# The aggregates' part of a candidate gate as seven block products, with new planner durations and a scrap tile that goes

## Chip, cores and metric

One core of one Trainium2 chip runs the whole program. The metric is the time of one execution on the device, in microseconds (us); the kernel before takes 2567.4 us, the median of three runs (2566.71 to 2567.45). All data are 32-bit floats, the adjacency matrices integers.

## The reference

128 graphs of 128 nodes with 256 features pass three graph attention layers, each added to its input, and a gated graph network of three steps. Cut to what matters here:

```python
# three attention layers (W, a of their own)
h = jnp.maximum(_layernorm(x, axis=-1), 0.0)
Wh = jnp.einsum('bnf,fo->bno', h, W)
e = (Wh @ a1)[:, :, None] + (Wh @ a2)[:, None, :]
e = jnp.where(e > 0, e, ALPHA * e)
attention = softmax(jnp.where(adj > 0, e, NEG_BIG), axis=-1)
x = x + elu(jnp.einsum('bij,bjo->bio', attention, Wh))     # layer 2 also times the node mask

# the gated network
h = jnp.maximum(_layernorm(x, axis=-1), 0.0)
for i in range(3):
    m = jnp.einsum('bnd,de->bne', h, weight[i])
    aggr = jnp.einsum('bst,bsd->btd', A, m)                 # A = (adj != 0)
    i_r, i_z, i_n = split(aggr @ w_ih.T + b_ih)
    h_r, h_z, h_n = split(h @ w_hh.T + b_hh)
    r, z = sigmoid(i_r + h_r), sigmoid(i_z + h_z)
    n = tanh(i_n + r * h_n)
    h = (1.0 - z) * n + z * h
return x + h
```

## The kernel before

**Tiling.** The graphs are cut into 33 groups: two graphs in the first and the last, four in the others. A group of four has 4 x 128 = 512 columns. In the gated network the state lies with features on the 128 partitions, as two blocks of 128 features (`k`), and the nodes of the group along the columns; `H` is half of the columns, `D` = 256. Groups 2 to 30 turn tiles by a DVE transpose and a trip through DRAM (`exchanged`, `turned_state`), the first two and the last two by products with an identity on TensorE. Each group runs three attention layers (`attention`), then three steps of the gated network (`step`), then its output.

**A step.** `aggregate` sums the neighbours' states (`agp`), and ACT copies the sum into `ag`. The matrices `weight[i]` and `w_ih` are multiplied in the set-up, so that the gates use `WC[i]` on `ag` and `WHH` on the state `h`. A product of a 256 x 256 matrix with a 256 x 512 tile, which as plain blocks is eight products of 128 x 128 with 256 columns, is done with seven: the tile is cut into blocks, `sums` (DVE) makes four differences of them (`t13`, `t24`), the set-up's `combinations` (POOL) made the matching sums of the matrix blocks, and ACT and DVE add up the partial results between the products, inside PSUM banks. `gates` does so for r and z (banks `a`, `e`, `b`), for the state's part and the aggregates' part alike, both into the same banks. `hidden_n` does it for the state's part of the candidate (banks `nn`, `nnb`) and leaves it in `wn`. The aggregates' part of the candidate goes another way: `candidate(c)` has DVE write (r + 1) x `wn` into a bank `ni`, lets TensorE add two plain 512-wide products onto it, and takes the Tanh from there. `kept_share` and `mixed` (in the last step `last_mixed`) make the new state. The r gate is used as tanh of half its argument, hence the factors of 0.5 and 0.25.

**Banks and buffers.** PSUM has eight banks, dealt out in rings: "gat" 2 (attention), "gru" 3 (`a`, `e`, `nn`), "seed" 2 (`b`, `nnb`, `ni`), "tr" 1. A tile of a ring is taken in turn; who wants a tile waits until all users of the tile that had it before are done. `wn` has four buffers (two taken by each step, with the first product of `hidden_n`), the input and residual tile `x` six, `em` (the attention matrix) two; the products of the scores with the vectors `VA` need an output that nobody reads, `scr`, with two buffers of its own.

**The order.** Nothing is left to a scheduler of the compiler: the class `Plan` collects all operations with an engine, a cost in us, a rank (a due time) and what they read and write, then `issue` plays them through as if they ran and so sets the order of every engine's instructions and of SP's DMAs. On each engine it takes, of the operations that can start first (within `WINDOW`), the one of lowest rank; operations whose rank is more than `AHEAD` (`EARLY` while the lowest rank is below `UNTIL`) above the lowest one left are held back. `LAG` is the time from an operation's end on one engine to its user on another. `pe`, `dve`, `act` and `pool` give costs by column count. Ranks come from the tables `ATT` (a group's three layers and the entry into the gated network), `STARTS` (its three steps), beyond the tables from a period of 3.0 ranks a group, and `SETUPS` for the set-up. The instructions then run on the chip when their data are there, in that order on each engine. DMAs all go through SP's queue.

## Time and profile before

The profiled execution took 2566.74 us; its span, from the first to the last instruction, is 2565.0 us.

| view | what | value |
|---|---|---|
| runs | median of three | 2567.4 us |
| profiled execution | time / span | 2566.74 / 2565.0 us |
| granted clock of TensorE | mean over the span | 0.993 |
| busiest group of PE | `hp`, attention's second product | 356.2 us |
| next | `ni`, the aggregates' part of the candidate (L1047) | 352.9 us, 792 instructions |
| DVE | score products L610 | 270.3 us |
| ACT | Tanh of the candidate L1052, 512 wide | 127.7 us, 687 ns each |
| POOL | power for the norms L528, 4 wide | 137.9 us, 1112 ns each |
| chain that ended last | share of PE | 95% |
| DMA | mean rate over the span | 96 GB/s |

PE is TensorE, PEld its weight loads, DVE the vector engine, ACT the scalar engine, POOL GpSimd, SP the engine that issues the DMAs. A 32-bit product appears as two instructions in the trace. A row of a group reads: line, engine, operation, output <- inputs, shapes, count, then busy time and mean ns of one, then the engine's rest just before such an instruction and what ended it. A line of waits reads: who <- what ended the wait, us in all, how many times, the longest. The mean of one instruction is its own length; since instructions overlap in an engine's pipe, a queue of them is spaced more closely than that.

### The profile page before, as it was taken

What the parts mean: (1) busy time and instruction counts of PE and PEld (TensorE: products, weight loads), DVE (VectorE), ACT (ScalarE), POOL (GpSimd) and SP (SyncE); (2) the same over time, 40 slices, a digit from 0 to 9 for tenths busy, and PEclk for the clock granted to TensorE, in tenths of its full rate; (3) what the DMA queues carried; (4) which work ended last, traced back from release to release, by engine and by line L of the source; (5) the groups of instructions that cost most, each with busy time, mean ns of one, the idle gap of its engine ahead of it and who ended that gap; (6) DMA issues with size and microseconds to landing.
All of it is one profiled execution on the core that took longest, in us unless ns stands there. A gap on an engine that the chain in (4) does not pass through costs nothing.

```text
span 2565.0 us, 39018 instructions
## 1 busy us (share of the span) xinstructions
PE 2527.7 (99%) x12549; PEld 2098.6 (82%) x12549; DVE 2105.9 (82%) x4955; ACT 1768.5 (69%) x4411; POOL 225.1 (9%) x328
## 2 busy tenths in 40 slices
PE   8799999999999999999999999999999999999998
PEld 5688888888888888888888888888888888888887
DVE  6778888888888888888888888888888888888765
ACT  6777676776766776766776666776666777666554
POOL 2210000000000000000000000000000000000000
PEclk8899999999999999999999999999999999999999
DMA  3113343343343333343334333333334443333320
GB/s 106 46 57 97 87 111 108 95 108 95 106 109 99 107 104 95 108 107 103 105 102 96 109 104 106 104 100 100 107 103 104 107 99 101 101 89 97 75 62 13
DMA packets 503123, 245.75 MB, mean 96 GB/s; under 512 B 280579, under 2 KB 472067, under 8 KB 502918
## 3 DMA queue, kind: packets, MB, share of 16 engines
q1 hardware_dynamic: 502918, 243.25, 35.3%
q8 instruction: 100, 1.64, 0.3%
q14 instruction: 105, 0.86, 0.1%
HBM read 139.28 MB, written 103.87 MB: 95 GB/s over the span
## 4 chain that ended last, share of the span: by engine, by line
PE 95%; DVE 2%; ACT 2%; DMA 1%; issue 0%; SPq 0%; POOL 0%; ACTq 0%; DVEq 0%
PE b L965 19%; PE hp L742 13%; PE e L965 13%; PE ni L1047 13%; PE a L965 13%; PE ahp L723 7%; PE agp L991 6%; PE nn L952 6%; PE nnb L952 5%; ACT em L666 0%; DVE scr L610 0%; ACT em L679 0%; PE hnp L852 0%; DMA at<-d_at 0%; ACT hn L791 0%
## 5 line engine op out<-in xcount | busy, mean ns | idle before, releaser
L742 PE MATMUL hp<-w,ah 128*128 128x256 f32 x1536 | 356.2, 384 | 0.5 <-ACT ah L730 0.5
L1047 PE MATMUL ni<-ag,wc_n 128*128 128x512 f32 (+1 forms) x792 | 352.9, 580 | 0.9 <-DVE ni L1041 0.9
L742 PEld LDWEIGHTS hp<-w,ah 128*128 128x128 f32 x1536 | 286.7, 191 | 61.9 <-ACT ah L730 13.1
L610 DVE SCALAR_TENSOR_TENSOR scr<-xn,va 128x256 f32<-128x256 f32 x732 | 270.3, 418 | 36.1 <-ACT xn L602 35.8
L1047 PEld LDWEIGHTS ni<-ag,wc_n 128*128 128x128 f32 x792 | 147.1, 190 | 125.2 <-issue 104.0
L756 ACT ACTIVATE t<-hp 128x512 f32<-128x512 f32 x192 | 104.6, 595 | 201.3 <-PE hp L742 201.2
L1052 ACT ACTIVATE wn<-ni,bi 128x512 f32<-128x512 f32 (+1 forms) x198 | 133.4, 674 | 157.5 <-PE ni L1047 114.5
L991 PEld LDWEIGHTS agp<-am,hn 128*128 128x128 f32 x1536 | 204.7, 191 | 42.7 <-issue 30.8
L991 PE MATMUL agp<-am,hn 128*128 128x128 f32 x1536 | 208.9, 275 | 3.6 <-ACT ag L999 3.0
L525 POOL TENSOR_SCALAR ve<-st 128x4 f32<-128x4 f32 (+1 forms) x132 | 28.4, 215 | 2087.8 <-DVE st L519 1735.5
L965 PE MATMUL a<-h,whh_rz 128*128 128x256 f32 (+1 forms) x792 | 208.8, 373 | 0.8 <-ACT z L1035 0.5
L723 PEld LDWEIGHTS ahp<-at,xn 128*128 128x128 f32 x1536 | 190.6, 196 | 23.0 <-issue 14.4
L602 ACT ACTIVATE xn<-x,nm,rs 128x256 f32<-128x256 f32 x366 | 201.1, 594 | 3.8 <-DVE nm L531 3.8
L965 PE MATMUL a<-ag,wc_rz 128*128 128x256 f32 (+1 forms) x792 | 199.1, 373 | 0.0
L723 PE MATMUL ahp<-at,xn 128*128 128x128 f32 x1536 | 192.5, 279 | 4.6 <-DMA at<-d_at 2.8
L758 DVE SCALAR_TENSOR_TENSOR x<-hp,x 128x512 f32<-128x512 f32 x192 | 124.0, 685 | 71.0 <-ACT t L756 70.9
L519 DVE BATCH_NORM_STATS2 st<-x 128x6 f32<-128x512 f32 x256 | 170.3, 690 | 2.6 <-DMA x<-in_x_dram 2.5
L649 ACT ACTIVATE em<-er,e 128x128 f32<-128x128 f32 x366 | 164.3, 523 | 2.4 <-DMA er<-de 2.3
L666 ACT ACTIVATE em<-em,nmx 128x128 f32<-128x128 f32 x384 | 149.4, 392 | 11.6 <-DVE nmx L662 11.4
L965 PEld LDWEIGHTS a<-h,whh_rz 128*128 128x128 f32 x792 | 140.9, 191 | 16.9 <-issue 0.7
L965 PEld LDWEIGHTS a<-ag,wc_rz 128*128 128x128 f32 x792 | 141.1, 191 | 15.2 <-issue 0.5
L528 POOL TENSOR_TENSOR rs<-ve,mhalf 128x4 f32<-128x4 f32 (+1 forms) x132 | 144.0, 1091 | 11.0
(158 smaller groups left out, 5541.3 us busy)
## 6 DMA issues: line engine op xcount, KB each, us to landing
d_hn<-tr_hn SPq DMA_DIRECT2D x116, 256.0 KB, 2.4
hn<-d_hn SPq DMA_DIRECT2D x464, 64.0 KB, 2.3
er<-de SPq DMA_DIRECT2D x90, 256.0 KB, 3.9
d_at<-tr_at SPq DMA_DIRECT2D x90, 256.0 KB, 2.2
at<-d_at SPq DMA_DIRECT2D x360, 64.0 KB, 2.0
x<-in_x_dram SPq DMA_DIRECT2D x31, 512.0 KB, 5.0
d_h<-tr_h SPq DMA_DIRECT2D x31, 512.0 KB, 2.7
h<-d_h SPq DMA_DIRECT2D x124, 128.0 KB, 2.7
```

Source lines behind the costliest of these rows:

```text
L519: add("DVE", dve(T), rank, lambda: nc.vector.bn_stats(st.t[:, b, :].rearrange("p b s -> p (b s)"), xt.t[:, b, :].rearrange("p b d -> p d b ...
L528: add("POOL", 1.04, rank, lambda: nc.gpsimd.tensor_tensor(rs.t, ve.t, mhalf[:, :n], op=OP.pow), reads=[ve], writes=[rs])
L602: add("ACT", 0.45, rank, lambda: nc.scalar.activation(xn.t[:, b, :], xt.t[:, b, :], AF.Relu, bias=nm.t[:, b : b + 1], scale=rs.t[:, b : b ...
L610: add("DVE", dve(D), rank, lambda: nc.vector.scalar_tensor_tensor(scr.t, xn.t[:, b, :], 1.0 if far else rs.t[:, b : b + 1], VA[l].t[:, s, ...
L649: add("ACT", 0.55 if far else 0.42, rank, lambda: nc.scalar.activation(em.t[:, b, :], e2_row(b), AF.Prelu, bias=e.t[:, 0, b : b + 1], alph ...
L666: add("ACT", 0.42, rank, lambda: nc.scalar.activation(em.t[:, b, :], em.t[:, b, :], AF.Exp, bias=nmx.t[:, b : b + 1], accum_out=sm.t[:, b ...
L723: add("PE", pe(P), rank, lambda: nc.tensor.matmul(summed(ps, b), xn.t[:, b, k * P : (k + 1) * P], turned_weights(b), start=True, stop=True ...
L742: add("PE", pe(D), rank, lambda: nc.tensor.matmul(hp.t[:, b * D : (b + 1) * D], ah.t[:, k, c * P : (c + 1) * P], W[l].t[:, k, :], start=(k ...
L952: op = add("PE", pe(H), at, lambda: nc.tensor.matmul(ps.t[:, o : o + H], WHH[1].t[:, blk, :], rhs(), start=starts, stop=True, skip_group_c ...
L965: nc.tensor.matmul(ps.t[:, gate * D : gate * D + H], w[0].t[:, blk, gate * P : (gate + 1) * P], rhs(), start=go, stop=w is not WHH, skip_g ...
L991: nc.tensor.matmul(ps.t[:, b * P : (b + 1) * P], s, am.t[:, b, :], start=True, stop=True)
L1047: add("PE", pe(TG), rank + 0.45 + 0.05 * c, lambda k=k: nc.tensor.matmul(ni[c].t[:, :TG], WC[i][1].t[:, k, c * P : (c + 1) * P], ag.t[:, k ...
```

## The change

**The candidate.** `input_n` is new. It does the aggregates' part of the candidate as seven products of `H` columns with blocks of `WC[i][1]` and the sums `ba_` that exist for r and z. It uses a bank `nx` of the ring "gru" and a bank `ny` of the ring "seed"; ACT copies one partial result to SBUF (`s7c`) and one within `nx`, DVE adds twice into `ny`. `candidate` now keeps (r + 1) x `wn` in `wn`, adds the finished bank to it with a second DVE operation and takes the Tanh from `wn`. The two banks `ni` of a step are gone. The set-up makes five more combinations for each of the three matrices and keeps seven 128-column blocks where it kept two of 256.

```diff
@@ -946,13 +971,14 @@
-            def one(ps, o, blk, what, at, starts, takes=()):
-
-                rhs, rkey = bh_[what]
+            def one(ps, o, blk, what, at, starts, takes=(), of_input=False, after=()):
+
+                w, (rhs, rkey) = (WC[i][1], ba_[what]) if of_input else (WHH[1], bh_[what])
                 op = add("PE", pe(H), at, lambda: nc.tensor.matmul(
-                    ps.t[:, o : o + H], WHH[1].t[:, blk, :], rhs(),
+                    ps.t[:, o : o + H], w.t[:, blk, :], rhs(),
                     start=starts, stop=True, skip_group_check=True,
-                ), reads=[WHH[1], rkey], writes=[ps], after=gone, takes=[*takes, *wn])
+                ), reads=[w, rkey], writes=[ps if starts else (ps, o)], after=[*gone, *after],
+                    takes=[*takes, *wn])
@@ -1032,26 +1058,50 @@
+            def input_n():
+
+                at = rank + 0.41
+
+                def reads(o):
+                    return [(nx, o)]
+
+                one(nx, 0, 0, "11", at, True, takes, True, list(begun))
+                one(nx, D, 6, "t3", at, False, (), True)
+                add("ACT", act(H), quick, lambda: nc.scalar.copy(s7c.t[:, :H], nx.t[:, D : D + H]),
+                    reads=reads(D), writes=[s7c])
+                add("ACT", act(H), quick, lambda: nc.scalar.copy(
+                    nx.t[:, D : D + H], nx.t[:, :H]), reads=reads(0), writes=reads(D))
+                one(nx, D, 5, "t2", at + 0.01, False, (), True)
+                one(nx, 0, 1, "21", at + 0.02, False, (), True)
+
+                def sum_with(o, after=()):
+                    return add("DVE", dve(H), quick, lambda: nc.vector.tensor_add(
+                        ny.t[:, o : o + H], nx.t[:, D : D + H], s7c.t[:, :H]),
+                        reads=[(nx, D), s7c], writes=[(ny, o)], after=after)
+
+                seeded.append(sum_with(0, copies))
+                one(nx, D, 4, "t1", at + 0.03, False, (), True)
+                sum_with(D)
+                one(ny, 0, 3, "t4", at + 0.04, False, (), True)
+                one(nx, D, 2, "22", at + 0.05, False, (), True)
+
             def candidate(c):
-                op = add("DVE", dve(TG), quick, lambda: nc.vector.scalar_tensor_tensor(
-                    ni[c].t[:, :TG], r[c].t[:, :TG], 1.0, wn[c].t[:, :TG], op0=OP.add, op1=OP.mult
-                ), reads=[r[c], wn[c]], writes=[ni[c]])
-                if c == 0:
-                    seeded.append(op)
-                for k in range(KD):
-                    add("PE", pe(TG), rank + 0.45 + 0.05 * c, lambda k=k: nc.tensor.matmul(
-                        ni[c].t[:, :TG], WC[i][1].t[:, k, c * P : (c + 1) * P], ag.t[:, k, :TG],
-                        start=False, stop=(k == KD - 1), skip_group_check=True,
-                    ), reads=[WC[i][1], (ag, k)], writes=[ni[c]])
+                add("DVE", dve(TG), quick, lambda: nc.vector.scalar_tensor_tensor(
+                    wn[c].t[:, :TG], r[c].t[:, :TG], 1.0, wn[c].t[:, :TG], op0=OP.add, op1=OP.mult
+                ), reads=[r[c], wn[c]], writes=[wn[c]])
+                ps = (ny, nx)[c]
+                add("DVE", dve(TG), quick, lambda: nc.vector.tensor_add(
+                    halves(wn[c].t), wide(ps.t), halves(wn[c].t)
+                ), reads=[ps, wn[c]], writes=[wn[c]])
                 cn = 2 * KD + c
-                add("ACT", act(TG) + 0.05, quick, lambda: nc.scalar.activation(
-                    wn[c].t[:, :TG], ni[c].t[:, :TG], AF.Tanh, bias=bi.t[:, cn : cn + 1]
-                ), reads=[ni[c], bi], writes=[wn[c]])
+                add("ACT", act(TG) + 0.1, quick, lambda: nc.scalar.activation(
+                    wn[c].t[:, :TG], wn[c].t[:, :TG], AF.Tanh, bias=bi.t[:, cn : cn + 1]
+                ), reads=[wn[c], bi], writes=[wn[c]])
```

**The scores' scrap.** `em` is taken before the scores, and the scores write the output that nobody reads into two rows of `em`; the tile `scr` is gone.

```diff
+        em = val(gw, "em", [G, N], f"em_{name}", cut=n)
         def score(b, s):
-            scr = val(gw, "scr", [D], f"scr_{name}_{b}_{s}")
+            rows = [(2 * s + r) % n for r in range(2)]
...
-            ), reads=[(xn, b), rs, VA[l]], writes=[scr, (e, (s, b))])
+            ), reads=[(xn, b), rs, VA[l]], writes=[(e, (s, b)), *((em, r) for r in rows)])
```

**Buffers.** `x` goes from 6 to 5, `wn` from 4 to 3 (`NB`), `s7n` from 1 to 2 (shared in turn with `s7c`), `t13a` from 1 to 2; `sums` takes only its own pair of tiles and no longer both pairs.

**The planner.** Every duration gets a new value, and the model new terms: a lag between dependent operations of one engine (`SELF`), an addition by the engine that waits (`TO`), a start-up after a wait of PE (`RESUME`). The tables of due times `ATT` (now 15 rows), `STARTS`, `SETUPS` and `LATE` (in place of `LEAD`, `SPAN`, `HEAD`) are new throughout, so the order of instructions changes everywhere.

```diff
-    LAG = {"PE": 0.26, "DVE": 0.2, "ACT": 0.2, "POOL": 0.15}
-    WINDOW = 0.097
-    AHEAD = 4.12
-    EARLY = 5.00
-    UNTIL = -1.46
+    LAG = {"PE": 0.2, "DVE": 0.117, "ACT": 0.137, "POOL": 0.035}
+    SELF = {"PE": 0.0, "DVE": 0.116, "ACT": 0.14, "POOL": 0.083, "SP": 0.0}
+    TO = {"PE": 0.27, "POOL": 0.05}
+    RESUME = 0.1
+    WINDOW = 0.01066
+    AHEAD = 6.09312
+    EARLY = 7.59896
+    UNTIL = 4.25807
...
     def pe(cols):
-        return 0.006 + cols / 600
+        return (0.0098 if cols < D else 0.0054) + cols / 600
     def dve(cols):
-        return 0.145 + cols / 960
+        return 0.069 + cols / 960
     def act(cols):
-        return 0.25 + cols / 1400
+        return 0.048 + cols / 1180
     def pool(cols):
-        return 0.35 + cols / 512
+        return 0.13 + cols / 390
...
-    URGENT = 1.00
+    URGENT = 0.61527
...
-    RB, ZB, NB, HB, H0 = 2, 2, 4, 2, 2
+    RB, ZB, NB, HB, H0 = 2, 2, 3, 2, 2
     NNR = 0.25
-    LEAD = 8.5
+    LATE = [-7.03390, -5.18110, -2.39000, 0.01170]
...
     def stage(g, l):
-        return ATT[g][l] if g < len(ATT) else 3.0 * g - LEAD + (SPAN * l if l < 3 else HEAD)
+        return ATT[g][l] if g < len(ATT) else 3.0 * g + LATE[l]
```

Two due times are moved by hand as well: the DMAs of `turned_state` come at the step's rank less 1.0, apart from the transposes ahead of them, and the transposes of the output (`later` in `exchanged`) at 1.0 less `URGENT` after theirs.

## The prediction

> **What bounds the kernel now.** I read the page's busy shares and slices first, then the stretches, then the waits of TensorE in the long middle, then the chain that ended last for the price of a product.
>
> ```profile
> PE 2527.7 (99%) x12549; PEld 2098.6 (82%) x12549; DVE 2105.9 (82%) x4955; ACT 1768.5 (69%) x4411; POOL 225.1 (9%) x328
> ```
>
> ```profile
> 0.00:128.00 128.00, 101.83 (x487) 76.40 (x488) 90.32 (x273) 88.78 (x259) 34.20 (x57) 0.88 0.26 76
> ...
> 320.00:2240.00 1920.00, 1918.05 (x9421) 1597.26 (x9421) 1628.07 (x3784) 1350.76 (x3342) 158.79 (x225) 1.00 0.39 103
> 2240.00:2565.00 325.00, 317.63 (x1632) 263.74 (x1630) 229.87 (x498) 188.13 (x461) 15.58 (x24) 0.99 0.26 69
> ```
>
> Columns: stretch, its length, then busy time of PE, weight loads, DVE, ACT and POOL, granted clock, DMA. In the middle 1920 us PE rests for 2 us at clock 1.00; 26 us of its 37 us of rest lie in the first 128 us. So in the middle the time is the sum of the products, and only there is a saved column a saved microsecond. DVE is busy for 85% there (1628/1920), ACT for 70%. The waits of PE between 330 and 2490 us are these, all of them:
>
> ```profile
> PE agp L991 <- ACT ag L999: 0.7, 1, 0.7
> PE e L965 <- DVE t13h L929: 0.4, 1, 0.4
> PE nn L952 <- ACT z L1035: 0.4, 1, 0.4
> PE ni L1047 <- DVE ni L1041: 0.3, 1, 0.3
> PE a L965 <- ACT b L1099: 0.3, 1, 0.3
> ```
>
> **The change, part by part.** The price of products, from the chain in order of time (start, length, instructions; each f32 product is two):
>
> ```profile
> 1212.72 3.43 PE ni L1047 x8
> ...
> 1230.88 1.73 PE b L965 x8
> ...
> 2507.52 0.89 PE e L965 x8
> ...
> 2510.63 1.73 PE ni L1047 x8
> ```
>
> *Removed and added on PE.* A full step has four 512-wide `ni` products, 3.43 us. It gets seven 256-wide ones; eight instructions of that width are four products and take 1.73 us, so seven take 7 x 0.4325 = 3.03 us. Gain 0.40 us. The DVE row of L1041 counts 186 full and 12 half forms, two a step: 93 full steps and 6 half. A half step goes from 1.73 to 7 x 0.89/4 = 1.56, gain 0.17. Sum: 93 x 0.4025 + 6 x 0.17 = **38.5 us**. The weight loads go from 8 to 14 a step, 190 ns each in their row, under 216 ns of a 256-wide instruction (1.73/8), so they stay hidden.
>
> In sentences that the sum can do without: per 256 columns the rows give 0.4325 us narrow and 3.43/8 = 0.429 us wide. The Trainium skill, "Perfetto Trace Analysis", Optimizing Tensor Performance, says that larger matmuls are the more efficient ones, which speaks against this cut. The rows agree, but at 4 ns a product: priced as if narrow products cost no more, the gain would be some 41 us, by the rows it is 38.5.
>
> *Added on DVE.* `candidate` keeps its 512-wide product (into `wn`, no longer into a bank) and gets a 512-wide add of a bank; `input_n` has two 256-wide adds. Nearest rows (bank and SBUF in, two tensors):
>
> ```profile
> L1106 DVE TENSOR_TENSOR e<-b,s 128x512 f32<-128x512 f32 x93 | 63.6, 684 | 7.9 <-PE b L965 6.4 <-ACT em L679 0.8 <-ACT s L1103 0.5
> L1022 DVE TENSOR_TENSOR nn<-nnb,s7n 128x256 f32<-128x256 f32 x93 | 39.9, 429 | 36.5 <-ACT wn L1008 36.2
> ```
>
> Per step 2 x 0.684 + 2 x 0.429 = 2.23 us alone. Queued behind others they cost less, as the order of time shows (start, length):
>
> ```profile
> 1207.80 1.30 DVE L1041 SCALAR_TENSOR_TENSOR ni<-r,wn 128x512 f32<-128x512 f32 x2
> 1209.01 0.69 DVE L1058 SCALAR_TENSOR_TENSOR h<-z,h 128x512 f32<-128x512 f32 x1
> ...
> 2509.49 0.43 DVE L1041 SCALAR_TENSOR_TENSOR ni<-r,wn 128x256 f32<-128x256 f32 x1
> 2509.82 0.42 DVE L1058 SCALAR_TENSOR_TENSOR h<-z,h 128x256 f32<-128x256 f32 x1
> ```
>
> Starts are 1.21/2 = 0.60 us apart at 512 and 0.33 to 0.34 at 256: 1.88 us a step. Over 96 full-step equivalents 180 to 214 us; I take the lower, as the queue will be dense. A group (three steps, three layers) takes 76.7 us now (the middle issues 4.91 PE instructions a us, and a group has 378) and would take 75.5. DVE's 65.0 us (85% of it) become 70.6 to 71.7, 94 to 95%. DVE is thus not the bound by its sum, but its rest falls from 11.7 to about 4.5 us a group.
>
> *Added on ACT.* Two 256-wide copies a step (rows of L1015 and L1017, 359 and 382 ns): 0.74 x 96 = 71 us, 70% to 74%. The candidate's Tanh reads SBUF instead of a bank; the nearest row of that kind, `cap` from SBUF, has 723 ns against 687, at most 7 us. ACT has 30% of rest, so I cost both at nothing; were there none, it would be 78 us.
>
> *A wait taken away.* Today the candidate runs Tanh of r, DVE product, two PE products (1.72 us plus whatever PE has queued before them), Tanh, DVE. All of PE's part now hangs on `ag` alone and can be done long before; between r and the Tanh stands a 0.60 us add. DVE waits today 46.7 us for `z L1081 <- ACT wn` and 39.6 us for `h L1070 <- ACT wn`, 86 of its 459 us of rest: room that the added work can use, and a shorter step behind it.
>
> *Waits and holds added.* (1) The "gru" ring has 3 banks and is taken four times a step instead of three; `nx` holds one until `candidate(1)` has added it. Behind a product that waits for a bank stands all of PE. (2) `wn` has 3 buffers instead of 4, so a step's first `nn` product, which takes both, stands behind the former step's `mixed(0)`. In the stretch I read, `nn` starts at 1235.06, the former step's `z` product at 1238.18: that order isn't possible any more, and PE needs 3 to 4 us of other work there. It has it: aggregation, the attention products (5.3 us in a layer) and the gates. (3) `em` is taken at the scores instead of at the Prelu; the ring of two is shared by three layers in 75 us. (4) `x` has 5 buffers instead of 6; a late load would delay statistics that run whole groups ahead. The lower bound of these is nothing, since PE has other work; the upper is the second rival. I take 3 us, near today's 2 us of waits, for the middle. Second buffers of `t13a` and `s7n` and the separated `takes` loosen waits that the middle doesn't show, so at nothing; if the added DVE work needs them, that is their worth and is in those 3 us.
>
> *The planner's new durations and due times* issue nothing; they reorder everything, DMAs on SP too. Where the former ones stood: a 512-wide DVE operation at 0.678 us against 0.60 seen, now 0.602. In the middle nothing can be gained by order (2 us of rest). In the head it can: bounds from -10 (a good part of 26 us) to +8. What is added there is POOL's five combinations for each of three weights, at 452, 453, 527 and twice 458 ns 2.4 us, or 7 us together, and six ACT copies of 296 ns. The last combination ends now at 74 us, the first recurrent product starts at 101 us: that slack hides them, but the power for a layer's statistics can stand 2.4 us behind a block of them. I take 0 for the head. In the tail, the 1.15 us of `ni` that stand alone on the chain at 2542.9 and 2556.2 each become a 0.43 us add: -2 with what follows.
>
> *Sum*, against the profiled execution's own 2566.7 us (span 2565.0): 2566.7 - 38.5 + 3 + 0 - 2 = 2529.2; the median of the runs is 0.7 above that execution, so **2530 us**.
>
> **The rivals.**
> (a) *The head or the tail gets better as well*: 2515 to 2520 (8 to 10 us of the 26). For it: PE's rest there. Against: the chain there is made of single dependent steps on all engines. 0.10.
> (b) *DVE becomes the bound*, slower than before. Its place is the middle: PE stands at a product whose bank or operand waits in DVE's queue. In 320 us of today's middle (12.5 steps) DVE works 271.4 and rests 48.6 us; with 12.5 x 2.23 = 28 us more it works 299. If its rest can't fall under half of today's (24 us), the stretch takes 323 instead of 320, and 2400 us of such stretches cost 25 us: 2592. It decides from a rest of 21 us, 7% of the stretch, where the gain is used up. For it: much of the rest is waiting for ACT and PE inside one chain, and more adds lengthen those chains (`nx` copy, product, add, product). Against: the 86 us that go with the `ni` products, and a PE that lost nothing at 85%. 0.18, reaching from 2575 to 2640.
> (c) *The gain is partly eaten* by the same waits or by the rings: 2542 to 2562, around 2550, 10 to 30 us of them. 0.11. At its end it is *no change*, 2562 to 2572: 0.05.
>
> In the head, the stretch from 72 to 80 us has 3.7 us of PE work and a granted clock of 0.56, and the next 8 us have 0.59. The Trainium skill, "TensorE: Matmul & The Clock Gate", Part 1, puts this down to a gate that halves the clock after an idle window of about 3.4 us. By it rival (b) would cost more than its waits only if single gaps grew that long; by rows of the middle (longest 0.7 us) they don't, and then only the waits count.
>
> **How the numbers follow.** Forecast (2520 to 2542) 0.56, (a) 0.10, (c) 0.11, no change 0.05, (b) 0.18. What this kernel's measurement can tell from no change is 0.2%, 5 us. Faster 0.56 + 0.10 + 0.11 = 0.77; within 0.05; slower 0.18. The range takes in (a), (c) and most of no change: 2512 to 2569, which leaves out (b) and a little. The likeliest's own range is 2520 to 2542: 8 of the bounds of head and mid to either side, and a few us more above, as DVE is nearly full.
>
> **What would show it.** Right: seven products at 0.43 us apart in place of `ni`; PE over 99% busy in the middle; a group in 75.5 us; DVE at 92 to 95% there; the waits of `z` and `h` for `wn` shorter. Wrong: PE waits of tens of us on `nx`, `ny`, `nn` or `b` with DVE or ACT as releaser; a first recurrent product much later than 101 us; a clock under 1.00 in the middle. A DVE whose rest stays above 21 us in 320 while PE waits would refute the forecast.

## The result and the profile after

The kernel after takes **2610.1 us** (median of four runs, 2606.9 to 2611.9) against 2567.4 for the kernel before: ratio **1.0165 [1.0148, 1.0183]**, slower by 43 us where 37 us of gain were forecast. The profiled run's span went from 2565.0 to 2605.1 us. The first page's busy times, and the chain that ended last by engine, of the kernel after:

```profile
PE 2517.8 (97%) x13143; PEld 2208.1 (85%) x13143; DVE 2214.2 (85%) x5351; ACT 1816.7 (70%) x4615; POOL 237.1 (9%) x343
...
PE 65%; DVE 15%; DMA 7%; ACT 6%; issue 4%; SPq 2%; POOL 1%; DVEq 0%; ACTq 0%; POOLq 0%
```

PE executes fewer microseconds than before and yet is the chain for only 65% of the span (95% before): DVE, transfers and ACT have entered it. The same four stretches as before, kernel after:

```profile
0.00:128.00 128.00, 103.62 (x511) 79.11 (x512) 88.41 (x277) 89.22 (x270) 41.83 (x69) 0.89 0.25 70
128.00:320.00 192.00, 181.61 (x995) 159.32 (x994) 162.52 (x422) 137.84 (x354) 19.02 (x25) 1.00 0.30 82
320.00:2240.00 1920.00, 1883.43 (x9760) 1661.27 (x9759) 1682.95 (x4017) 1368.13 (x3443) 157.28 (x221) 1.00 0.38 102
2240.00:2605.00 365.00, 349.10 (x1884) 308.35 (x1882) 280.32 (x637) 221.49 (x551) 18.98 (x28) 0.99 0.27 70
```

The head is as it was. In the middle PE rests 36.6 us in 1920 where it rested 2, at the same clock of 1.00. A group of four graphs has 378 + 18 = 396 PE instructions now; at 9760/1920 = 5.083 a microsecond it takes 77.9 us, against 378/(9421/1920) = 77.0 before. What PE waits for, kernel after, whole run, the first four lines (who <- what ended the wait, us, times, longest):

```profile
PE ahp L743 <- DMA at<-d_at: 38.4, 37, 2.6
PE e L658 <- DVE em L631: 11.0, 12, 3.8
PE nx L977 <- DVE ny L1083: 6.6, 11, 1.3
PE nx L977 <- ACT nx L1077: 4.3, 4, 1.7
```

The first line is new: in 37 attention layers PE stands at `ahp` (attention times features) because the attention matrix, turned by DVE and a trip through DRAM, isn't back. Before, this wait was 2.8 us in 2 places:

```profile
PE ahp L723 <- DMA at<-d_at: 2.8, 2, 2.0
```

**Work and standing still.** Busy time of PE is modelled where products overlap, so I also added up starts. Unhindered, PE's instructions of 128, 256 and 512 columns start 0.111, 0.216 and 0.429 us apart; the sum of these is PE's work, and whatever lies between two starts beyond it is standing still (products that run at a lower clock count in it too). Worked out from the traces so (us; standing still by stretch; the wait lists above are shorter, since part of a stall falls on the weight load ahead of the product):

| kernel | PE's work | 0–128 | 128–320 | 320–2240 | later | standing still |
|---|---|---|---|---|---|---|
| before | 2490.3 | 48.8 | 3.5 | 7.2 | 7.8 | 67.3 |
| after | 2451.2 | 48.6 | 16.0 | 60.5 | 21.7 | 146.8 |

The work fell by 39.1 us; standing still rose by 79.5. The difference, 40.4, is the rise of the span (40.1). Of the 79.5 us, `ahp` has 45.6 (10.9 to 56.5), the `nx` and `ny` products together some 28 (30.4, less 2.3 at the old `ni`), `e` in the groups with identity products 9.6.

**The room of a trip.** The transfers themselves are not slower: `d_at<-tr_at` lands 2.3 us after its issue (2.2 before), `at<-d_at` 2.0 (2.0 before). What changed is when PE comes for the result. There are 93 trips, three layers of each group from the third on; the last two groups turn this matrix by the trip as well. For trips 15 to 79, where the trace recorded the last return's landing, I took the time from that landing to the first `ahp` product:

| kernel | trips | median us | one in ten below | below 0.35 us |
|---|---|---|---|---|
| before | 39 | 2.35 | 1.70 | 0 (least 0.93) |
| after | 44 | 0.23 | 0.14 | 27 |

Where PE waited, it mostly started 0.13 us after the landing. So before, every one of these trips had some 0.8 us or more to spare; after, most have next to none. A stall of the kernel after in its chain, which is followed back from the product (start, length, what):

```profile
1267.24 0.69 DVE e L1156
1267.93 0.61 DVE tr_at L566
1268.55 0.03 DVE em L631
1268.57 2.03 DMA d_at<-tr_at
...
1271.52 0.42 SPq L577
1271.95 0.04 issue
1271.99 3.22 DMA at<-d_at
1275.21 0.14 issue
1275.34 2.02 PE ahp L743 x16
```

The chain doesn't run along PE here: it goes from DVE's queue through the transpose, the way out, SP's issue of four reads and the way back, 7.4 us from transpose to product, and the fourth read took 3.22 us where the median is 2.0. The planner of after counts 1.6 us and the size for a landing, 0.7 us less for the way out; in its plan 6.9 us pass in the median from the transpose's start to `ahp`, on the chip 7.3 (the same trips, 15 to 79), and 8.1 or more in one layer of four.

### The profile page after: what moved, and what is told of

Read it like the earlier page. It is cut to its first block, busy times and chain, and to the rows that moved or that the text cites. A ratio compares the mean times of both kernels' runs of the same rounds, so it can differ in the third digit from the quotient of the medians.

```text
span 2605.1 us, 40605 instructions
## 1 busy us (share of the span) xinstructions
PE 2517.8 (97%) x13143; PEld 2208.1 (85%) x13143; DVE 2214.2 (85%) x5351; ACT 1816.7 (70%) x4615; POOL 237.1 (9%) x343
## 4 chain that ended last, share of the span: by engine, by line
PE 65%; DVE 15%; DMA 7%; ACT 6%; issue 4%; SPq 2%; POOL 1%; DVEq 0%; ACTq 0%; POOLq 0%
PE b L991 13%; PE hp L762 10%; PE a L991 8%; PE e L991 8%; PE nx L977 7%; PE ahp L743 6%; PE agp L1017 4%; PE nn L977 4%; DMA d_at<-tr_at 3%; PE nnb L977 3%; DMA at<-d_at 3%; DVE em L631 2%; SPq L577 2%; PE ny L977 1%; ACT em L686 1%
## 5 line engine op out<-in xcount | busy, mean ns | idle before, releaser
L762 PE MATMUL hp<-w,ah 128*128 128x256 f32 x1536 | 363.4, 381 | 1.0 <-ACT ah L750 1.0
L631 DVE SCALAR_TENSOR_TENSOR em<-xn,va 128x256 f32<-128x256 f32 x732 | 279.2, 419 | 13.5 <-ACT xn L616 12.6
L991 PE MATMUL a<-h,whh_rz 128*128 128x256 f32 (+1 forms) x792 | 220.8, 375 | 0.0
L539 POOL TENSOR_SCALAR ve<-st 128x4 f32<-128x4 f32 (+1 forms) x132 | 36.0, 273 | 1984.4 <-DVE st L533 1786.9
L1094 DVE SCALAR_TENSOR_TENSOR wn<-r,wn 128x512 f32<-128x512 f32 (+1 forms) x198 | 133.6, 675 | 94.7 <-ACT r L1061 94.2
L669 ACT ACTIVATE em<-er,e 128x128 f32<-128x128 f32 x366 | 174.4, 522 | 25.7 <-DMA er<-de 24.7
L1102 ACT ACTIVATE wn<-wn,bi 128x512 f32<-128x512 f32 (+1 forms) x198 | 137.4, 706 | 67.5 <-DVE wn L1098 67.1
L977 PE MATMUL nx<-ag,wc_n 128*128 128x256 f32 (+1 forms) x594 | 177.1, 380 | 3.4 <-DVE ny L1083 2.5
L750 ACT COPY ah<-ahp 128x512 f32<-128x512 f32 (+1 forms) x198 | 112.0, 569 | 77.6 <-PE ahp L743 77.2
L1025 ACT COPY ag<-agp 128x512 f32<-128x512 f32 (+1 forms) x198 | 112.3, 567 | 72.9 <-PE agp L1017 70.0
```

The lines of the kernel that those rows point to most:

```text
L631: add("DVE", dve(D), rank, lambda: nc.vector.scalar_tensor_tensor(scr(), xn.t[:, b, :], 1.0 if far else rs.t[:, b : b + 1], VA[l].t[:, s, ...
L669: add("ACT", 0.418 if far else 0.25, rank, lambda: nc.scalar.activation(em.t[:, b, :], e2_row(b), AF.Prelu, bias=e.t[:, 0, b : b + 1], alp ...
L762: add("PE", pe(D), rank, lambda: nc.tensor.matmul(hp.t[:, b * D : (b + 1) * D], ah.t[:, k, c * P : (c + 1) * P], W[l].t[:, k, :], start=(k ...
L977: op = add("PE", pe(H), at, lambda: nc.tensor.matmul(ps.t[:, o : o + H], w.t[:, blk, :], rhs(), start=starts, stop=True, skip_group_check= ...
L991: nc.tensor.matmul(ps.t[:, gate * D : gate * D + H], w[0].t[:, blk, gate * P : (gate + 1) * P], rhs(), start=go, stop=w is not WHH, skip_g ...
L1094: add("DVE", dve(TG), quick, lambda: nc.vector.scalar_tensor_tensor(wn[c].t[:, :TG], r[c].t[:, :TG], 1.0, wn[c].t[:, :TG], op0=OP.add, op1 ...
```

## The experiments

Two theories at the start. **T**: the products' gain is there; the new durations are the medians of what the chip does, the due times were made for them, and the order thus fixed leaves late transfers and late links (from one operation's end to its user's start) no room; each lateness is paid by PE and never won back. **D** (the forecast's rival b): DVE is too full. Times that follow are medians on the chip; ratios are to the kernel before on the same chip.

**e1, the wait for the trip taken away** (kernel after, order unchanged; the sum over neighbours is left out):

```diff
-                return at.t[:, :, : n * 32].rearrange("p q (b c) -> p b q c", b=n)[:, b]
+                return ident.rearrange("p (q c) -> p q c", q=Q)
```

> The changed kernel with the same order, but the neighbour sums of the attention layers take an identity tile as their moving operand in place of the turned attention matrix, which is still sent through DRAM: the product no longer waits for that trip (the sum over neighbours is left out). Theory T (the planner puts the product at the moment at which it reckons the trip to end, the trip is often longer, and TensorE, in its fixed order, stands still): the 38 us of waits of ahp for at<-d_at go and nothing takes their place, 2560 to 2578 us. Theory D (DVE, nearly full, runs late and these waits are only where the lateness shows): the waits move to other products, 2595 us or more.

Measured 2578.3 us, 1.0036 [1.0023, 1.0049]. By the ratios, 33 of the 43 us go with one wait; the value lies just at the upper end of what T expected. In the profiled executions (e1's slowest, after's fastest) standing still falls by 25 us, from 146.8 to 121.7: `ahp` has 50 us less, but half of that moves on, to `hp` above all (17.1 us, 3.2 in after), so "nothing takes their place" held only in part. D would have left the time above 2595.

**e2, the candidate's added DVE sums made narrow** (kernel after, order unchanged; most of the aggregates' part of the candidate is left out):

```diff
-                    halves(wn[c].t), wide(ps.t), halves(wn[c].t)
+                    halves(wn[c].t)[:, :, :32], wide(ps.t)[:, :, :32], halves(wn[c].t)[:, :, :32]
```

> The changed kernel with the same order, the two new adds of candidate() on 32 of 256 columns of each half (most of the input's part of the candidate is left out). Some 0.47 us of DVE work less for each, 90 us in all, half of what the change added. Theory D: DVE's lateness halves, 2580 us or less. Theory T: DVE isn't what the products wait for, 2600 to 2612 us, with the waits of ahp for at<-d_at as they were.

Measured 2604.9 us, 1.0144 [1.0127, 1.0161]: 5 us less, with 70 us of DVE work gone. Its busy times, and below them its longest wait of PE:

```profile
PE 2512.1 (97%) x13143; PEld 2212.5 (85%) x13143; DVE 2144.2 (82%) x5351; ACT 1816.6 (70%) x4615; POOL 236.6 (9%) x343
```

```profile
PE ahp L743 <- DMA at<-d_at: 42.4, 40, 2.7
```

DVE has a load near that of before, and the trips are as late as ever. That speaks against D.

**e3, only the planner's landing time raised by 0.8 us** (kernel after, ordered anew, same due times):

```diff
-                op.lands = moved - op.end + 1.6 + op.more
+                op.lands = moved - op.end + 1.6 + op.more + 0.8
```

> The changed kernel, whose planner reckons every DMA to land 0.8 us later than it did (2.4 in place of 1.6); due times unchanged, so the order is another. Theory T: with room for the longer trips the waits for at<-d_at fall to a few us and the time to 2555 to 2585 us, although the due times weren't made for this. Theory D: 2600 us or more, since DVE's work is the same.

Measured 2596.7 us, 1.0106 [1.0091, 1.0121]. Half a hit: the room of the trips rises to a median of 1.41 us, and standing still at `ahp` falls to 10.8 us, as before the change. But only some 15 us are gained; the head has 53.1 us now, and by starts `b`, `a`, `e` and `nx` have 13, 11, 24 and 31 us where they had 4, 1, 18 and 28 in after. T's time of 2555 to 2585 was missed, and D's 2600 too, by 3 us: a margin alone doesn't mend due times that were made without it.

**e4, the new durations, lags and holding bounds on the kernel before** (no due time and no instruction altered; cut):

```diff
-    LAG = {"PE": 0.26, "DVE": 0.2, "ACT": 0.2, "POOL": 0.15}
+    LAG = {"PE": 0.2, "DVE": 0.117, "ACT": 0.137, "POOL": 0.035}
...
-                op.lands = moved - op.end + 1.9 + op.more
+                op.lands = moved - op.end + 1.6 + op.more
...
-        return 0.145 + cols / 960
+        return 0.069 + cols / 960
```

> The kernel before with nothing of the change but the planner's durations and lags (products, scrap tile, buffers and due times as before). Theory T: the durations as the trace shows them take away the room that the longer ones left: waits for at<-d_at come, 2580 to 2620 us. Theory D: DVE has no more to do than before, 2567 us within 5.

Measured 2624.1 us, 1.0213 [1.0198, 1.0228]: 55 us lost with not one instruction added, and the time 4 us above T's upper bound. PE's work is before's 2490.3, standing still 125.5 us (67.3 before), 26.5 of it at `ahp`; DVE has less to do than before (the page's line), and the trip's wait leads PE's list:

```profile
PE 2549.2 (97%) x12549; PEld 2110.8 (80%) x12549; DVE 2042.7 (78%) x4955; ACT 1760.8 (67%) x4411; POOL 224.2 (9%) x328
```

```profile
PE ahp L731 <- DMA at<-d_at: 12.4, 9, 3.6
```

**e5, DVE's load alone** (kernel before, order unchanged; the three operations likewise):

```diff
-                op = add("DVE", dve(TG), quick, lambda: nc.vector.scalar_tensor_tensor(
+                op = add("DVE", dve(TG), quick, lambda: [nc.vector.scalar_tensor_tensor(
...
-                ), reads=[r[c], wn[c]], writes=[ni[c]])
+                ) for _ in range(2)], reads=[r[c], wn[c]], writes=[ni[c]])
```

> The kernel before, in its own order, with three of VectorE's operations of each step run twice, with the same result: the sum of the state's half, the sum for the hidden candidate, and the product of reset gate and hidden candidate (0.40 + 0.40 + 0.68 us, in each of 99 steps, the last one twice: about 1.9 to 2.2 us of VectorE more in each step, some 185 to 210 us in all, as much as the change adds). Nothing else is altered. Theory D (VectorE so full that TensorE is held up by it): 2600 us or more, with waits of TensorE for VectorE of over 30 us. Theory T (an order made for the medians has no room for late transfers, VectorE's load is not the cause): the order of before has room, so within 15 us of 2569, at most 2584, with the waits of TensorE for the attention's transposed operand below 15 us.

Measured 2618.6 us, 1.0198 [1.0182, 1.0213], so T's expectation of at most 2584 was missed, and D's 2600 or more was met; PE's waits that DVE ended come to 25.1 us, short of the 30 that D asked for. The waits say what kind of loss it is; of TensorE, the first lines:

```profile
PE nnb L952 <- DVE wn L1025: 11.4, 42, 1.4
PE atp L695 <- ACT ah L730: 3.4, 1, 3.4
...
PE ahp L723 <- DMA at<-d_at: 2.4, 2, 2.1
```

Standing still rose by 52.0 us, and 34.9 of that are at `nnb<-h` (2.0 to 36.9 us), the product right behind a doubled operation: in each step PE stands up to 0.4 us before the first of its two instructions and 0.1 us before the second. Most of the rest is at two other products behind doubled operations, `ni` (8.1) and `nnb<-t13h` (7.7). Trips are in time as before. What is paid is links a few tenths of a us longer than the fixed order counted. So the run doesn't separate T and D as it was meant to (it lengthens links and the load at once); it shows how dear a small link is when the order is fixed. PE's busy share of the middle, 99%, says nothing against D here:

```profile
320.00:2240.00 1920.00, 1907.22 (x9259) 1558.98 (x9259) 1750.56 (x4011) 1330.57 (x3290) 162.45 (x221) 1.00 0.38 101
```

PE started 9259 instructions there against 9421 before, 33 us less work. The run that rules D out is e10, with DVE as full as here.

**e6, the new candidate and scrap on the old planner** (the edits of the change without durations and due times; cut):

```diff
+            em = val(gw, "em", [G, N], f"em_{name}", cut=n)
...
+            input_n()
             candidate(0)
```

> The candidate's seven products and the scrap in the mask tile, with the buffers that they need, ordered by the planner of before: its durations, lags and due times, none of the new ones. Theory S (the new products save their 39 us in any order that has room, and only the new durations do harm): 2530 to 2575 us. Theory T2 (the due times are a part of the kernel too: they were made for one set of instructions, and a changed set without new ones loses more than the products save): over 2600 us, with TensorE's work near 2451 us as in the kernel after and the rest in its waits, above all in those where the attention's operations stand late in the order.

Measured 2839.6 us, 1.1057 [1.1040, 1.1073], with PE's work at after's 2451.2 and 379 us of standing still, most of it at `nx` (118) and the other products of the gates. T2 right, S wrong: with the old due times the new set of instructions loses far more than it saves. Its middle stretch and one of its waits also show what gaps do to the clock:

```profile
320.00:2240.00 1920.00, 1817.81 (x9042) 1562.72 (x9042) 1592.47 (x3728) 1280.70 (x3171) 151.25 (x204) 0.97 0.35 94
```

```profile
PE ahp L735 <- DMA at<-d_at: 23.4, 6, 8.5
```

The granted clock of the middle is 0.97; in after, with no wait there over 2.6 us, it stayed at 1.00. The trace's clock records put 122 us of e6's middle at half clock. Of these, 27 us begin in or just behind gaps of 3.1 to 8.5 us. The other 95 us begin where no single gap was longer than 1.7 us, but two or three came within some 5 us; one such place, with PE's longest wait between 1325 and 1345 us:

```profile
1333.40:1343.60 10.20, 8.86 (x23) 6.52 (x24) 5.01 (x9) 4.37 (x10) 0.00 (x0) 0.50 0.35 104
```

```profile
PE nx L969 <- ACT nx L1069: 1.4, 1, 1.4
```

The Trainium skill, "TensorE: Matmul & The Clock Gate", Part 1, has a window of about 3.4 us of idling before the clock is halved. The first 27 us are near that rule; the other 95 us don't fit it, so here keeping every single gap short was not enough.

**e7, the scrap in the mask tile alone** (kernel before):

```diff
-            scr = val(gw, "scr", [D], f"scr_{name}_{b}_{s}")
+            rows = [(2 * s + r) % n for r in range(2)]
...
-            ), reads=[(xn, b), rs, VA[l]], writes=[scr, (e, (s, b))])
+            ), reads=[(xn, b), rs, VA[l]], writes=[(e, (s, b)), *((em, r) for r in rows)])
```

> The kernel before with only the scores' scrap written into the mask tile, ordered anew by its own planner with its own durations and due times; no product is altered. It takes the mask tile from the first score on, a few us earlier than the masking did. Theory S (the earlier hold costs nothing, as the prediction had it): within 8 us of 2569. Theory T2 (with due times made for another set of instructions, the earlier claim of the buffer reorders the work): 2600 us or more, with no wait for the mask tile itself needed to explain it but waits of TensorE spread over attention and gates.

Measured 2636.1 us, 1.0263 [1.0246, 1.0280]. PE's work is unaltered; standing still is 136.8 us, 64.0 of it in the head; 50 of it are gaps of over 2 us at scattered places. So the earlier claim of one buffer, costed at nothing, costs 67 us as long as the due times were made without it.

**e10 and e11, the change with other due times** (every instruction of after; the planner's numbers chosen anew, by trying many orders against transfers as late as the traces show them, in two separate searches; cut, e10):

```diff
-    LAG = {"PE": 0.2, "DVE": 0.117, "ACT": 0.137, "POOL": 0.035}
+    LAG = {"PE": 0.37153, "DVE": 0.11451, "ACT": 0.14138, "POOL": 0.035}
...
-                op.lands = moved - op.end + 1.6 + op.more
+                op.lands = moved - op.end + 2.57096 + op.more
...
-    LATE = [-7.03390, -5.18110, -2.39000, 0.01170]
+    LATE = [-6.42341, -4.78754, -2.08545, -0.83050]
...
-        return STARTS[g][i] if g < len(STARTS) else 3.0 * g + [0.0, 2.00000, 4.00000][i]
+        return STARTS[g][i] if g < len(STARTS) else 3.0 * g + [0.00000, 1.96011, 3.74634][i]
```

> The change as it is, every instruction of the kernel after, with only the planner's numbers chosen anew: a longer landing for transfers (2.4 instead of 1.6 us, about), with due times tried out against late transfers as the traces show them, not against medians. Theory T (the cost is lateness in a fixed order, the structure is sound): 2545 to 2575, TensorE's work near 2451 us as in after, its standing still under 110 us, the waits for the returned matrix under 15 us. Rival B (rings of banks, fewer buffers or VectorE's load hold the new structure back in any order): 2590 or more.

> As the run before it, with another set of due times found in the same way from another start, to tell whether one order was luck. Theory T: 2545 to 2580, both orders within 15 us of each other. Rival B: 2590 or more.

Measured **2557.2 us, 0.9955 [0.9943, 0.9968]** for e10, faster than both kernels (by 11 us than before on the same chip), and 2576.3 us, 1.0027 [1.0017, 1.0038], for e11, faster than after but 8 us slower than before. Both are within T's bounds and far from B's 2590; the 15 us that they were to differ at most became 19. The busy times, the middle stretch and the waits of PE of e10, one view after the other:

```profile
PE 2497.0 (98%) x13143; PEld 2214.5 (87%) x13143; DVE 2226.9 (87%) x5351; ACT 1804.3 (71%) x4615; POOL 227.0 (9%) x343
```

```profile
320.00:2240.00 1920.00, 1914.46 (x10007) 1707.00 (x10006) 1740.91 (x4145) 1396.47 (x3532) 154.19 (x227) 1.00 0.39 104
```

```profile
PE hTp L826 <- ACT hn L811: 7.2, 1, 7.2
PE e L658 <- DVE em L631: 5.5, 8, 1.3
...
PE ahp L743 <- DMA at<-d_at: 2.5, 2, 1.9
```

The same instructions, with DVE at 91% of the middle, and PE rests for 5.5 us there (13.7 by starts). A DVE this full thus doesn't hold PE up by itself: D falls. A group takes 396/(10007/1920) = 76.0 us. Trips have a median room of 5.19 us (2.02 in e11, and there 37 us are lost in the middle). By the same sums as above:

| kernel | PE's work | 0–128 | 128–320 | 320–2240 | later | standing still |
|---|---|---|---|---|---|---|
| e3 | 2451.2 | 53.1 | 16.7 | 46.5 | 17.8 | 134.0 |
| e10 | 2451.2 | 56.5 | 9.6 | 13.7 | 16.9 | 96.8 |
| e11 | 2451.2 | 55.4 | 8.4 | 37.0 | 16.1 | 116.9 |

**e8 and e9, trips made later, a first attempt** (kernels before and after; order unchanged):

```diff
+                for j in range(2):
+                    nc.sync.dma_start(spare[j], ident[:1, :64])
             nc.sync.dma_start(d.t.rearrange("q r j f -> (q r) j f"), tr.t[:, :, :f])
```

> The kernel before, same order; ahead of every transfer that takes the attention matrix out to DRAM (d_at), SP issues two further transfers of 256 bytes that nobody reads. By the spacing of SP's issues in these traces (0.44 to 0.53 us) the matrix comes back some 0.9 us later in each of some 90 trips; no product and no order is altered. Theory T (the order of before leaves the trip room, the order of after leaves it none): the room is 1.2 to 1.4 us in the median, so most trips are still in time: 2568 to 2585. Rival R (a trip's delay is paid wherever it is, 90 x 0.9 us = 81 us, or none is, since other work covers it): 2630 or more, or 2569 here and no rise in the companion run either.

> The kernel after, same order, with the same two transfers of 256 bytes ahead of every transfer of the attention matrix to DRAM. Theory T: a trip that is late already pays the whole 0.9 us, those in time by less than that a part of it: with 37 late trips at least 33 us, with all 90 at most 81 us more than after's 2610, so 2643 to 2691, nearly all of the rise in TensorE's waits for the returned matrix. Rival R: a rise like that of the companion run on before.

Measured 2568.4 us, 0.9999 [0.9990, 1.0009], and 2625.2 us, 1.0215 [1.0201, 1.0229]. The pair doesn't test what it was meant to: SP issued the small transfers while it waited for the transpose anyway, and from transpose to first read the median stayed at 2.8 us in before, and went from 2.63 to 2.69 in after. T's 2643 to 2691 for after was missed. The 13 us or so by which after rose (1.0215/1.0165) stand at `ahp` (14 us more by starts); they probably come from the trips behind which SP had no rest.

**e12 to e14, trips made later, in earnest** (before, after, e10; order unchanged). The small transfers read the transposed tile and thus can't go ahead of it:

```diff
+                for j in range(3):
+                    nc.sync.dma_start(spare[j], tr.t[:1, 0, :64])
             nc.sync.dma_start(d.t.rearrange("q r j f -> (q r) j f"), tr.t[:, :, :f])
```

> The kernel before, same order, with three further transfers of 256 bytes ahead of every transfer of the attention matrix to DRAM; they read the transposed tile, so SP can issue them only when the trip begins. At 0.3 us each (spacing of such transfers in the run e9) the matrix comes back some 0.9 us later in each of 93 trips. Theory T (room of 1.2 to 1.4 us): 2568 to 2585 us. Rival R (a delay is paid in full wherever it is): about 2569 + 93 x 0.9 = 2652.

> The kernel after, same order, with the same three transfers. Theory T (no room): the 37 trips that TensorE waits for today pay 0.9 us each, others a part: 2643 to 2690. Rival R: as much as before loses in the companion run.

> The retimed order of e10 (2557 us), with the same three transfers. Its planner allows each transfer 0.97 us more than after's, two to a trip. Theory T: that room takes most of the 0.9 us: 2557 to 2590. If the retimed order owed its gain to something else and had no more room than after's, it would rise by at least 33 us, to 2590 or more.

| kernel | us | ratio to before | rise | transpose to way out | to the first read |
|---|---|---|---|---|---|
| e12, before | 2573.3 | 1.0015 [1.0005, 1.0024] | 4 us | 0.03 to 0.90 | 2.78 to 2.98 |
| e13, after | 2649.6 | 1.0317 [1.0300, 1.0334] | 39 us | 0.03 to 0.90 | 2.63 to 3.09 |
| e14, e10 | 2562.2 | 0.9972 [0.9961, 0.9983] | 4 to 5 us | 0.03 to 0.89 | 2.21 to 2.99 |

The rises are between ratios (1.0317/1.0165, 0.9972/0.9955), the last two columns medians from the traces, without and with the delay. The waits for the matrix in the three, in this order:

```profile
PE ahp L729 <- DMA at<-d_at: 3.2, 4, 1.7
```

```profile
PE ahp L749 <- DMA at<-d_at: 66.9, 58, 3.2
```

```profile
PE ahp L749 <- DMA at<-d_at: 4.0, 3, 2.9
```

All three lie within what T expected, 2649.6 near its lower edge. SP's queue gave part of the delay back, more in before than in e10: taken trip by trip, the first read came later by 0.39 us in the mean in before, 0.65 in after and 0.78 in e10. So 93 x 0.39 = 36 us of lateness cost 4 us in before, 60 us cost 39 in after, and 73 us cost 4 to 5 in e10. In after the whole rise stands at `ahp` (41 us more by starts; 4 more in e10). Lateness is paid for the greater part where PE comes as the trip lands, and hardly at all where it comes microseconds later.

**The plan against the chip.** `issue` plays the order through as if it ran, so each kernel's file also tells how long its own plan is. That separates two kinds of loss: an order that is long already in the plan, and an order that the chip can't keep up with.

| kernel | plan, us | span on the chip | chip later by |
|---|---|---|---|
| before | 2582.6 | 2565.0 | -17.6 |
| after | 2510.6 | 2605.1 | 94.5 |
| e3 | 2548.9 | 2592.3 | 43.4 |
| e4 | 2569.4 | 2623.4 | 54.0 |
| e6 | 2822.9 | 2837.0 | 14.1 |
| e7 | 2658.5 | 2634.5 | -24.0 |
| e10 | 2540.8 | 2555.2 | 14.4 |
| e11 | 2533.5 | 2575.7 | 42.2 |

In e6 and e7 the loss is in the plan: due times that don't fit the instructions. In after and e4 the plan is short and the chip is late. e11 is late too although its trips have room: trips are not the only links that need some.

## Why the prediction was wrong

**The products: right.** Forecast 38.5 us less work on PE; the sum over the starts fell by 39.1.

**The failed step** is the one that began "The planner's new durations and due times issue nothing; they reorder everything" and went on "In the middle nothing can be gained by order (2 us of rest)". The forecast asked what an order can win and put a bound on that. It set none on what an order can lose, though the change replaced every due time and took spare time out of most durations: landing 1.9 to 1.6 us and 0.7 us less again for the way out, DVE's base 0.145 to 0.069, lags 0.2 to 0.117 and 0.137 (only into PE they grew, from DVE 0.2 to 0.387). I had seen that the old DVE figure stood at 0.678 against 0.60 and read it as an error that is mended; with the landings it was room. From the issue of a trip's way out to its last landing the plan of before counts 7.33 us in the median, where the chip has 6.53, and 7.11 at nine in ten; the plan of after counts 5.73, where the chip has 5.99 and 7.43. The term "3 us for the middle" measured 53 (7.2 to 60.5), with 12.5 more in 128 to 320.

That the order is the cause is shown from both sides: the planner's new durations, lags and bounds alone lose 55 us (e4), and other planner numbers on the same instructions win 54 and 35 (e10 and e11 against after, by the ratios). That late trips are the largest single part is shown by e1 (33 us) and by e13 against e14. How the rest splits over the links at `nx`, `ny` and `e` was not tested one by one.

**Rival (b)** named a time that holds the result (2575 to 2640) for a reason that doesn't. It was to decide at a DVE rest of 21 us in 320; in after DVE rests (1920 - 1682.95)/6 = 39.5 us while PE waits, which the forecast had itself named as what would refute it. With 70 us of DVE's load taken away 5 us return (e2), and in e10 DVE rests 29.8 us in 320 with PE at 99.7%. What (b) had right is only that chains through DVE grew dear. Its remark on the clock, that only single gaps grown to an idle window would cost more than the waits, is too mild by e6's middle.

**DVE's load was over-sized**: 180 to 214 us expected, 94 to 95% of a group; the page has 108 us more (2105.9 to 2214.2), 88% of the middle and 91% in e10. The rows of the added operations, kernel after:

```profile
L1083 DVE TENSOR_TENSOR ny<-nx,s7c 128x256 f32<-128x256 f32 x186 | 79.9, 429 | 49.9 <-PE nx L977 31.4 <-PE ny L977 16.0 <-ACT em L699 0.9
L1098 DVE TENSOR_TENSOR wn<-ny,wn 128x512 f32<-128x512 f32 x93 | 63.7, 685 | 3.0 <-PE ny L977 2.3
L1098 DVE TENSOR_TENSOR wn<-nx,wn 128x512 f32<-128x512 f32 x93 | 63.4, 682 | 0.8 <-PE nx L977 0.4
```

Their lengths were priced rightly (429 and 684 ns) and sum to 207 us; the busy time is the union, and it depends on the order: the unchanged operations of before fill 2105.9 us there and 2042.7 in e4. That a denser queue overlaps more of them is the likely reason. **ACT**: 71 us expected, 48 more measured, at nearly no cost, as said (4.3 us of PE's waits in after end at one of the added copies).

**The wait that goes**: right. DVE's waits of `z` and `h` for the Tanh, 46.7 and 39.6 us before, are 2.7 and 3.4 us now. In their place DVE waits for the reset gate, the first line of its list in after:

```profile
DVE wn L1094 <- ACT r L1061: 94.2, 73, 4.4
...
DVE h L1120 <- ACT wn L1102: 3.4, 4, 1.0
...
DVE z L1131 <- ACT wn L1102: 2.7, 4, 0.8
```

**Head and tail**: 0 for the head was right (48.8 and 48.6); -2 for the tail was wrong, +13.9. **Rings and buffers**: costed at nothing from below. e7 shows that a buffer's earlier claim can cost 67 us through the order alone; e10, that with due times made for them all of these together cost little: 13.7 us in the middle against 7.2, near the 3 us of the forecast.

**Small slips in its sums**: 378 instructions at 4.91 a us are 77.0 us a group, not 76.7, and rival (a)'s 8 to 10 us off 2530 give 2520 to 2522, not 2515 to 2520. Neither bears on the outcome.

**What stays open.** With e10 the change is worth 11 us, not 37. Of the 39 us that the products save, 29.5 go into standing still beyond before's: 7.7 in the head, 6.1 in 128 to 320, 6.5 in the middle, 9.1 later; whether a better order exists for them wasn't tried further. Nor was the kernel before given new due times against the same lateness, so how much of e10's time it could reach by that alone is not known. The two searches ended 19 us apart: an order is a matter of luck to that extent, and e11 shows that new due times alone needn't bring the change out ahead of before.

## What to carry to other kernels

Where an order is fixed in advance and one engine is full, the durations that it was made with are not a description but the room that late work has: a plan with medians turns many arrivals into waits (37 of 93 trips here), and an engine without rest has nothing to win a lateness back from. Before costing a new order at nothing, measure for each long round trip how long its result lies ready before it is fetched, and keep that above the spread of the trip. Then compare the plan's own length with the chip's: a chip that runs late needs room, a plan that is long needs other due times. Any edit to the set of instructions or to a buffer's claim voids the due times; try it with due times of its own before judging it.

## What was not expected of the hardware

The trip through DRAM has a wide spread: from the issue of `d_at` to the landing of the last `at`, after has 5.99 us in the median, 7.01 at three in four, 7.43 at nine in ten; in before it is 6.53, 6.67, 7.11 (the 63 and 57 of 93 trips whose last landing was recorded). Transfers of 256 bytes leave SP about 0.3 us apart, reads of 64 KB 0.43 us. Putting three of them ahead of a trip's way out moved that by 0.86 to 0.87 us in all three kernels, and the median of the first read by 0.20, 0.46 and 0.78 us; how much of a delay arrives probably depends on what else stands in SP's queue.
